# Taking the accumulators of a 5x5 convolution out through ScalarE, with the image added by TensorE

## The chip, the cores and the metric

The kernel runs on one core of a Trainium2 chip. Its time is device microseconds for one launch, from the first to the last instruction of the program. The kernel before takes 4448.21 us, the median of three runs (4447.31 to 4449.51). The profiled execution, from which all the durations below come, took 4449.83 us, of which the profile's span covers 4448.0 us.

The core has five engines that work from separate queues, each strictly in the order in which the program wrote them: TensorE (PE; the profile shows its weight loads apart, as PEld), VectorE (DVE), ScalarE (ACT), GpSimd (POOL) and SyncE (SP), which issues most of the transfers.

## The reference, cut to what matters

Four images of 128 channels and 64x64 pixels go through four residual layers. Before each layer the image is normalised in groups of four channels (`_gn`), with mean and variance over the group's channels and pixels.

```python
x = x + attention(_gn(x))          # layer 0: q, k, v of 128 channels, 4096 pixels, softmax over all of them
x = x + conv5x5(_gn(x))            # layer 1: the 5x5 convolution, 128 -> 128 channels
x = x + state_space_scan(_gn(x))   # layer 2: forward and backward scans, 64 channels x 64 states each
x = x + conv3x3(_gn(x))            # layer 3: the 3x3 convolution, with a bias
```

The change concerns the end of layer 1: the convolution's result is added to the image, and the sum and the sum of squares of the new image are taken, from which layer 2's group norm follows.

## The kernel before, in words

**Two streams of work.** The scan of layer 2 is the longest piece. It is cut into ticks, 256 for an image (`TICKS`), so 1024 for four images. A tick covers 128 rows (32 channels times 4 states) and 1024 pixels. For a tick ScalarE makes the decays (`decay`, L1246), GpSimd multiplies the drive by a row of the input matrix (`drive`, L1253), VectorE runs the recurrence (`recur`, the scan at L1263), and the result is multiplied by a row of the output matrix, on VectorE (L1266) or, for the ticks that `to_pool` gives away, on GpSimd (`weigh`, L1284). TensorE sums the products over the states (`collect`, L1304). While the decays live in one bank of 512 pixels each, there are three such banks, so `decay` can't be further ahead of `recur` than that; when image 3's operands are all made, `widen` gives two banks of 1024 pixels in their place.

**What fills the ticks.** All other work is one chain of Python generators, `images()`: for each image the attention (`attention`), the 5x5 convolution (`conv_pairs`), the operands of its scan (`scan_prep`, `scan_operands`), and, after the fourth image's operands, the end of layer 2 and layer 3 of images 0 to 2 (`stage`, `scan_end`, `conv`). The loop over `scan_core` (L1552) writes half a tick of the scan, adds half of `pace` to a credit, and draws steps from `images()` until the credit is used up. A step gives back a cost by which it is charged: `PRODUCT` = 0.86 for a product on TensorE, `SLOT` = 0.7 for a slot of operands, `HOP` = 1.7 for other steps. `pace` is 2.8 a tick until image 3's operands are made, then `ENDPACE` = 1.5. So the scan of image b is written between the attention and convolution of image b+1.

**Where the two streams meet.** The scan of image b can't be written before its first operands are. `before(b)` (L1537) is called four ticks ahead; if the operands are late, it draws the missing steps of `images()` at once, with no tick between them (it drains them). At the very end `result()` (L1545) does the same for the last transfers of image 3. `to_pool` also looks at whether operands are being made at that moment.

**The convolution.** `conv_pairs` treats two image rows at once. For each of four pieces of 1024 pixels there are three accumulators in TensorE's output memory, of 512 pixels each: `pq`, which both rows share (10 products), and `pe0` and `pe1`, for the even and the odd row (15 products each). `lean` is true for images 1 to 3. In the lean form ScalarE copies `pq` into `qs` (L975), and a product of `qs` with the identity matrix adds it to `pe0` and to `pe1` (L989). A finished accumulator isn't taken out at once: `done()` is called after the third product of the next accumulator (L966), and after the last one following a step of `HOP`. It calls `add` (L928), where VectorE adds the accumulator to the image in place and gives the sum (L930); ScalarE then gives the sum of squares into `st2` (L934, recorded at L331). The images' first, not lean, form is used for image 0 alone and is the same in both kernels.

After the last `add`, `scan_prep` aggregates the sums on VectorE (L338 to L379), GpSimd makes the scale (L381, L382), ScalarE normalises (L387), and only then TensorE can begin the taps of the short convolution (L1044).

Of the kernel before, what the change touches and what calls it, by code (L numbers as in the profile page):

```python
# [26 lines left out]
AF = mybir.ActivationFunctionType  # L27
ALU = mybir.AluOpType
# [17 lines left out]
PRODUCT, HOP, SLOT, PACE, ENDPACE, AHEAD = 0.86, 1.7, 0.7, 2.8, 1.5, 4  # L46
# [6 lines left out]
def conv_preact_kernel(  # L53
# [16 lines left out]
    nc = tc.nc  # L70
# [45 lines left out]
    ident = const.tile([P, P], F32, name="ident")  # L116
# [711 lines left out]
    def conv_pairs(b, xs, tag, st, st2, lean):  # L828

        NP, CK = H // 2, CH // W // 2  # L830
        WQ = W + PAD
        xp = large(b, f"xpe_{b}")
        rows = xp[:, : HP * WQ].rearrange("p (h w) -> p h w", w=WQ)
        xh = xs.rearrange("p (h w) -> p h w", w=W)
        nc.gpsimd.memset(rows[:, :PAD, :], 0.0)
        nc.gpsimd.memset(xp[:, (HP - PAD) * WQ : HP * WQ + PAD], 0.0)
        nc.gpsimd.memset(rows[:, PAD : HP - PAD, :PAD], 0.0)
        gn = yield from group_norm(st, f"e{b}")
        diffs = pools["big"].tile([P, VSIZE], F32, tag="V", name=f"df_{b}")
        nc.gpsimd.memset(diffs[:, 2 * (NP + 1) * WQ :], 0.0)  # L840

        def by_rows(t, n):

            return [t[:, o : o + n * WQ].rearrange("p (h w) -> p h w", w=WQ) for o in (0, PAD)]

        def piece(i):
            h0, h1 = i * H // 4, (i + 1) * H // 4
            normalise(rows[:, PAD + h0 : PAD + h1, PAD:], xh[:, h0:h1, :], gn)

        def odd(j, n):  # L850
            nc.gpsimd.tensor_tensor(
                diffs[:, j * WQ : (j + n) * WQ].rearrange("p (h w) -> p h w", w=WQ),
                rows[:, 2 * j + 1 : 2 * (j + n) : 2, :], rows[:, 2 * j + 2 : 2 * (j + n) + 1 : 2, :],
                ALU.subtract,
            )

        def even(j, n):
            at = (NP + j) * WQ
            nc.gpsimd.tensor_tensor(
                diffs[:, at : at + n * WQ].rearrange("p (h w) -> p h w", w=WQ),  # L860
                rows[:, 2 * j + 1 : 2 * (j + n) : 2, :], rows[:, 2 * j : 2 * (j + n) - 1 : 2, :],
                ALU.subtract,
            )

        wide = pools.get("fill") if not lean else None
        if wide:
            NC = NP * WQ + PAD
            combos = wide.tile([P, 3, NC], F32, tag="combos", bufs=1, name="combos")
            nc.gpsimd.memset(combos[:, :, NP * WQ :], 0.0)
            views = [by_rows(combos[:, n, :], NP) for n in range(3)]  # L870

        def combine(j, n):
            for m, (p, q, op) in enumerate(
                ((1, 2, ALU.add), (0, 2, ALU.subtract), (3, 1, ALU.subtract))
            ):
                a, b_ = (rows[:, 2 * j + r : 2 * (j + n) + r - 1 : 2, :] for r in (p, q))
                nc.vector.tensor_tensor(views[m][0][:, j : j + n, :], a, b_, op)

        def differences(i):
            last = i == 3  # L880
            if wide:
                combine(8 * i, 8)
            odd(8 * i, 8 + last)
            even(8 * i + 1, 8 + last)

        padded, differ = by_rows(xp, HP), by_rows(diffs, 2 * (NP + 1))

        def image(r, dx):
            late = dx // PAD > 0
            dx -= late * PAD  # L890
            return padded[late][:, r : r + 2 * CK - 1 : 2, dx : dx + W]

        def diff(r, dx):
            late = dx // PAD > 0
            dx -= late * PAD
            return differ[late][:, r : r + CK, dx : dx + W]

        def combo(n):
            def view(r, dx):
                late = dx // PAD > 0  # L900
                dx -= late * PAD
                return views[n][late][:, r : r + CK, dx : dx + W]
            return view

        def chunk(t, c, y):

            v = t[:, bass.ts(c, CH)].rearrange("p (h t w) -> p h t w", t=2, w=W)
            return v[:, :, y, :]

        def flat(t):  # L910
            return t.rearrange("p (h w) -> p h w", w=W)

        piece(0)
        yield HOP / 2
        piece(1)
        differences(0)
        K5 = 5
        steps, done = [], None
        taps5 = more[0] if wide else exchange(b)[:, : NTAP * C].rearrange("p (k c) -> p k c", c=C)

        def matrix(w, dx):
            if w < SUM12:
                return taps5[:, w * K5 + dx, :]
            if w < HSUM:
                return cs[:, (w - SUM12) * K5 + dx, :]
            return more[1][:, w - HSUM, dx, :]

        def add(c, y, acc):  # L928
            i = 2 * c + y
            nc.vector.scalar_tensor_tensor(  # L930
                chunk(xs, c, y), flat(acc), 1.0, chunk(xs, c, y), ALU.mult, ALU.add,
                accum_out=st2.sum(i),
            )
            st2.squares(i, chunk(xs, c, y), xs[:, 0:1])  # L934

        for c in range(L // CH):
            j = c * CK
            if c < 2:
                piece(2 + c)
            if c < 3:  # L940
                differences(c + 1)
            accs = [
                (bank("s", f"pq_{b}_{c}"), ((SUM12, image, 2 * j + 2), (SUM34, image, 2 * j + 4))),
                (bank("a", f"pe0_{b}_{c}"),
                 ((0, image, 2 * j), (1, diff, j), (3, diff, j + 1))),
                (bank("z", f"pe1_{b}_{c}"),
                 ((0, image, 2 * j + 1), (2, diff, NP + j + 1), (4, diff, NP + j + 2))),
            ]
            if wide:
                total, first, last = (combo(n) for n in range(3))  # L950
                accs = [
                    (accs[0][0], (accs[0][1][1], (HSUM, total, j))),
                    (bank("y", f"pm_{b}_{c}"), ((HDIF, diff, j),)),
                    (accs[1][0], ((0, first, j), (3, diff, j + 1))),
                    (accs[2][0], ((2, last, j), (4, diff, NP + j + 2))),
                ]
            for n, (acc, parts) in enumerate(accs):
                k, total = 0, len(parts) * K5
                for w, view, r in parts:
                    for dx in range(K5):  # L960
                        k += 1
                        nc.tensor.matmul(  # L962
                            flat(acc), matrix(w, dx), view(r, dx),
                            start=k == 1, stop=k == total and (n == 0 or not lean),
                        )
                        if k == 3 and done is not None:  # L966
                            done()
                            done = None
                        if k % 3 == 0:
                            yield 3 * PRODUCT  # L970
                if n == 0:
                    qs = pools["bg"].tile([P, MM], F32, tag="w", bufs=4, name=f"q_{b}_{c}")

                    def done(acc=acc, qs=qs, c=c):
                        nc.scalar.copy(qs, acc)  # L975
                        for y in range(0 if lean else 2):
                            nc.gpsimd.tensor_tensor(
                                chunk(xs, c, y), chunk(xs, c, y), flat(qs), ALU.add
                            )
                    yield PRODUCT  # L980
                elif wide and n == 1:
                    def done(acc=acc, c=c):
                        for y, op in enumerate((ALU.subtract, ALU.add)):
                            nc.vector.tensor_tensor(
                                chunk(xs, c, y), chunk(xs, c, y), flat(acc), op
                            )
                else:
                    if lean:
                        nc.tensor.matmul(acc, ident, qs, start=False, stop=True)  # L989
                        yield PRODUCT  # L990

                    def done(acc=acc, c=c, y=n - len(accs) + 2):
                        add(c, y, acc)
        yield HOP
        done()
        ready.add((b, "convolved"))
# [379 lines left out]
    def program(safe):  # L1376
# [118 lines left out]
        with ExitStack() as es, tc.manual_schedule():  # L1495
# [49 lines left out]
            def result():  # L1545

                while (B - 1, "staged") not in ready:
                    next(work)
                return ends[B - 1][2]

            credit = 0.0
# [91 lines left out]
```

## Time and profile before

| | us |
|---|---|
| median of three runs | 4448.21 |
| profiled execution | 4449.83 |
| span of its profile | 4448.0 |
| PE busy in the span | 3922.3 (88%) |
| DVE busy | 3722.6 (84%) |
| POOL busy | 3637.1 (82%) |
| ACT busy | 2398.0 (54%) |

The busy times are averages over stages that differ. For this change the stages of the lean images count: for image 1 the products of attention start between 732 and 1365 us, those of the convolution between 1398 and 1560 us, and the operands are made from about 1567 to 1666 us; images 2 and 3 repeat that. From about 3550 us on the last scan runs with the ends of the other images.

A matmul of fp32 operands shows as two MATMUL records, each with a duration of some 0.59 us, and the next begins 0.43 us after the last: a product takes about 0.85 us of TensorE. Counts of PE records are therefore twice the number of products.

### The profile page before, as it was taken

What the parts mean: (1) busy time and instruction counts of PE and PEld (TensorE: products, weight loads), DVE (VectorE), ACT (ScalarE), POOL (GpSimd) and SP (SyncE); (2) the same over time, 40 slices, a digit from 0 to 9 for tenths busy, and PEclk for the clock granted to TensorE, in tenths of its full rate; (3) what the DMA queues carried; (4) which work ended last, traced back from release to release, by engine and by line L of the source; (5) the groups of instructions that cost most, each with busy time, mean ns of one, the idle gap of its engine ahead of it and who ended that gap; (6) DMA issues with size and microseconds to landing.
All of it is one profiled execution on the core that took longest, in us unless ns stands there. A gap on an engine that the chain in (4) does not pass through costs nothing. (4 is left out here: it accounts for less than half of the span.)

```text
span 4448.0 us, 43613 instructions
## 1 busy us (share of the span) xinstructions
PE 3922.3 (88%) x13480; PEld 1492.0 (34%) x13480; DVE 3722.6 (84%) x3703; ACT 2398.0 (54%) x4425; POOL 3637.1 (82%) x1728
## 2 busy tenths in 40 slices
PE   8999997999999979999999889999999657576666
PEld 4444433333333323333333333333333112121222
DVE  4722217999999978999999889999999899999995
ACT  3333226666665476666664576666654754444532
POOL 3433307999999978999999889999999899999995
PEclk9999999999999989999999989999999869787887
DMA  1000016545545565455545565455445666656562
GB/s 64 21 1 1 0 55 230 182 163 178 178 173 177 178 228 195 173 178 173 182 167 173 205 228 178 166 178 179 169 178 178 225 217 208 229 199 232 189 228 78
DMA packets 213171, 726.10 MB, mean 163 GB/s; under 512 B 25152, under 2 KB 26432, under 8 KB 212672
## 3 DMA queue, kind: packets, MB, share of 16 engines
q1 hardware_dynamic: 211328, 722.49, 46.0%
q8 instruction: 108, 1.77, 0.2%
q14 instruction: 135, 1.11, 0.1%
q10 hardware_dynamic: 1600, 0.73, 0.1%
HBM read 653.98 MB, written 69.14 MB: 163 GB/s over the span
## 5 line engine op out<-in xcount | busy, mean ns | idle before, releaser
L1253 POOL TENSOR_TENSOR db<-dx,br 128x1024 f32<-128x1024 f32 x1024 | 2398.3, 2365 | 219.5 <-DMA dx<-dxd 59.5
L1246 ACT ACTIVATE da<-de,a_neg 128x512 f32<-128x512 f32 (+1 forms) x1796 | 1343.9, 751 | 741.7 <-DVE da L1263 435.5
L482 PE MATMUL sc<-r,x 128*128 128x512 f32 x2048 | 1080.8, 610 | 11.1 <-ACT last L1279 5.2
L494 PE MATMUL acc<-exchange,v 128*128 128x512 f32 x2048 | 1050.2, 595 | 2.2
L1284 POOL TENSOR_TENSOR hc<-hc,cr 128x1024 f32<-128x1024 f32 x401 | 947.9, 2364 | 17.8 <-ACT last L1279 15.3
L1266 DVE TENSOR_TENSOR hc<-da,cr 128x512 f32<-128x512 f32 (+1 forms) x1078 | 835.5, 775 | 66.8 <-DVE da L1263 0.5
L488 ACT ACTIVATE exchange<-sc 128x512 f32<-128x512 f32 x1024 | 603.2, 589 | 513.6 <-PE sc L482 508.3
L1304 PE MATMUL y<-hc,sel 128*32 128x512 f32 x4096 | 606.4, 647 | 261.6 <-POOL hc L1284 248.7
L1263 DVE TENSOR_TENSOR_SCAN da<-da,last,db 128x512 f32<-128x512 f32 (+1 forms) x464 | 728.3, 1570 | 17.2 <-POOL db L1253 14.7
L1263 DVE TENSOR_TENSOR_SCAN da<-da,da,db 128x512 f32<-128x512 f32 x455 | 585.5, 1287 | 14.9 <-ACT da L1246 14.4
L482 PEld LDWEIGHTS sc<-r,x 128*128 128x128 f32 x2048 | 363.1, 190 | 579.7 <-issue 383.8
L494 PEld LDWEIGHTS acc<-exchange,v 128*128 128x128 f32 x2048 | 387.2, 190 | 499.5 <-issue 479.3
L1263 DVE TENSOR_TENSOR_SCAN hc<-da,last,db 128x512 f32<-128x512 f32 (+1 forms) x304 | 455.7, 1499 | 2.3 <-POOL db L1253 0.7
L1263 DVE TENSOR_TENSOR_SCAN hc<-da,hc,db 128x512 f32<-128x512 f32 x317 | 406.7, 1283 | 43.5 <-ACT da L1246 13.8
L536 POOL TENSOR_TENSOR sidep<-sidep,exchange 128x512 f32<-128x512 f32 x120 | 170.9, 1424 | 273.3 <-ACT exchange L488 271.0
L1304 PEld LDWEIGHTS y<-hc,sel 128*32 128x32 f32 x4096 | 114.6, 112 | 692.4 <-POOL hc L1284 342.1
L536 DVE TENSOR_TENSOR sided<-sided,exchange 128x512 f32<-128x512 f32 x120 | 95.9, 799 | 221.5 <-ACT exchange L488 220.1
L1263 DVE TENSOR_TENSOR_SCAN da<-da,db 128x512 f32<-128x512 f32 (+1 forms) x159 | 235.8, 1483 | 11.3 <-ACT da L1246 7.3
L696 PE MATMUL pcm<-xpm,cs 128*128 128x512 f32 x432 | 211.7, 639 | 35.8 <-ACT xpm L387 35.8
L516 PE MATMUL zp<-exchange,ones 128*32 128x512 f32 x1536 | 205.6, 600 | 11.6 <-DVE xs L583 11.6
L962 PE MATMUL pe<-df,exchange 128*128 128x512 f32 x480 | 213.7, 595 | 0.0
L1279 ACT COPY last<-da 128x1 f32<-128x1 f32 x474 | 73.9, 156 | 254.3 <-DVE hc L1266 251.8
(241 smaller groups left out, 2851.1 us busy)
## 6 DMA issues: line engine op xcount, KB each, us to landing
br<-bm SPq DMA_DIRECT2D x512, 512.0 KB, 5.2
cr<-cm SPq DMA_DIRECT2D x512, 512.0 KB, 3.9
de<-dd SPq DMA_DIRECT2D x64, 512.0 KB, 4.9
dx<-dxd SPq DMA_DIRECT2D x64, 512.0 KB, 6.4
x<-in_x_dram SPq DMA_DIRECT2D x16, 512.0 KB, 5.2
xs<-in_x_dram SPq DMA_DIRECT2D x16, 512.0 KB, 6.1
xsd<-xs SPq DMA_DIRECT2D x16, 512.0 KB, 6.5
xcd<-xc SPq DMA_DIRECT2D x16, 512.0 KB, 3.0
```

What stands on the lines that cost most here:

```text
L482: nc.tensor.matmul(sc, xn[:, bass.ts(j, P)], rq[blk], start=True, stop=True)
L488: nc.scalar.activation(pt, sc, AF.Exp)
L494: nc.tensor.matmul(acc[blk], v[:, j, :], ring[:, u % NRING, :], start=j == 0, stop=j == NJT - 1)
L536: eng.tensor_tensor(s, s, ring[:, u % NRING, :], ALU.add)
L696: nc.tensor.matmul(acc.rearrange("p (r w) -> p r w", w=W), weights[:, t, :], xp[:, y : y + RPM, dx : dx + W], start=t == 0, stop=t == k * ...
L962: nc.tensor.matmul(flat(acc), matrix(w, dx), view(r, dx), start=k == 1, stop=k == total and (n == 0 or not lean),)
L1246: nc.scalar.activation(da, rep["de", b, c, d, g][:, bass.ts(h, size)], AF.Exp, scale=a_neg[:, at(i)])
L1253: nc.gpsimd.tensor_tensor(dbs[i], rep["dx", b, c, d, g], rows["b", b, c, d, q], ALU.mult)
L1263: nc.vector.tensor_tensor_scan(h, da, db[:, cut], before, ALU.mult, ALU.add)
L1266: nc.vector.tensor_tensor(hc[:, cut], h, rows["c", b, c, d, q][:, cut], ALU.mult)
L1284: nc.gpsimd.tensor_tensor(hcs[i], hcs[i], rows["c", b, c, d, q], ALU.mult)
L1304: nc.tensor.matmul(y[r : r + SG, :], sel, hcs[first + gg][:, bass.ts(h, MM)], start=q == back, stop=False, tile_position=(0, r), skip_grou ...
```

## The change

In the lean form, which is that of images 1, 2 and 3, `add` no longer uses VectorE. TensorE adds the image itself to each accumulator, by one more product with the identity matrix, and ScalarE copies the accumulator over the image and gives its sum in the same instruction. The step that holds these products is charged for two of them. `result()` accepts that the generator ends while it draws from it.

```diff
         def add(c, y, acc):
             i = 2 * c + y
-            nc.vector.scalar_tensor_tensor(
-                chunk(xs, c, y), flat(acc), 1.0, chunk(xs, c, y), ALU.mult, ALU.add,
-                accum_out=st2.sum(i),
-            )
+            if lean:
+                nc.scalar.activation(
+                    chunk(xs, c, y), flat(acc), AF.Identity, accum_out=st2.sum(i)
+                )
+            else:
+                nc.vector.scalar_tensor_tensor(
+                    chunk(xs, c, y), flat(acc), 1.0, chunk(xs, c, y), ALU.mult, ALU.add,
+                    accum_out=st2.sum(i),
+                )
             st2.squares(i, chunk(xs, c, y), xs[:, 0:1])
...
                     if lean:
-                        nc.tensor.matmul(acc, ident, qs, start=False, stop=True)
-                        yield PRODUCT
+
+                        nc.tensor.matmul(acc, ident, qs, start=False, stop=False)
+                        nc.tensor.matmul(
+                            flat(acc), ident, chunk(xs, c, n - 1), start=False, stop=True
+                        )
+                        yield 2 * PRODUCT
...
                 while (B - 1, "staged") not in ready:
-                    next(work)
+                    next(work, None)
                 return ends[B - 1][2]
```

## The prediction

> **What bounds the kernel now.** I read the page first, its sums and its slices, to see which engines have room at all.
>
> ```profile
> PE 3922.3 (88%) x13480; PEld 1492.0 (34%) x13480; DVE 3722.6 (84%) x3703; ACT 2398.0 (54%) x4425; POOL 3637.1 (82%) x1728
> PE   8999997999999979999999889999999657576666
> DVE  4722217999999978999999889999999899999995
> POOL 3433307999999978999999889999999899999995
> ```
>
> From slice 7 on three engines are near full together; only ACT has room. The dips in slices 14-15, 22-23 and 31 are where the operands of images 1 to 3 are made. Next, the busy time by engine in the three lean convolutions.
>
> ```profile
> core 0: us, PE busy (x) PEld busy (x) DVE busy (x) ACT busy (x) POOL busy (x), PEclk, DMA share, GB/s
> 1398.00:1562.00 164.00, 162.49 (x514) 63.94 (x512) 157.55 (x166) 74.71 (x118) 160.13 (x72) 1.00 0.52 176
> 2345.00:2508.00 163.00, 162.76 (x526) 63.17 (x524) 156.17 (x164) 73.06 (x115) 158.97 (x71) 1.00 0.49 172
> 3287.00:3450.00 163.00, 161.16 (x513) 63.16 (x511) 157.58 (x166) 73.69 (x117) 159.69 (x72) 1.00 0.50 180
> ```
>
> PE is busy in 99% of it, POOL in 98%, DVE in 96%. For DVE I then read its waits in the first of them: all of them together are 2.2 us, so its missing 4% is the short space between dependent instructions, and DVE is full too.
>
> ```profile
> DVE hc L1263 <- ACT da L1246: 1.0, 3, 0.3
> DVE da L1263 <- ACT da L1246: 0.8, 1, 0.8
> DVE da L1263 <- POOL db L1253: 0.4, 1, 0.4
> ```
>
> Is PE really full, when its busy time is modelled? The timeline says so: between two groups of y (L1304), which come every four ticks, 12.38 us pass from 1545.13 to 1557.51; the 24 records between them at 0.43 us and the y group at 1.92 us make 12.3. A tick there takes 3.41 us (45 GpSimd drives in 153.4 us). Last I read the timeline where image 1's convolution ends.
>
> ```profile
> 1559.36 1.12 PE L989 MATMUL pe<-q,ident 128*128 128x512 f32 x2
> ...
> 1567.10 0.67 DVE L930 SCALAR_TENSOR_TENSOR xs<-pe,xs 128x512 f32<-128x512 f32 x1
> ...
> 1567.87 0.72 ACT L331 ACTIVATE junk<-xs,aw_s 128x512 bf16<-128x512 f32 x1 [2.54 <-DVE xs L930]
> ...
> 1568.71 0.17 DVE L338 TENSOR_REDUCE gn_sums<-su_s 128x2 f32<-128x16 f32 x1 [0.94 <-ACT junk L331]
> ...
> 1573.44 1.97 PE L1044 MATMUL pt<-xn,wtap 128*64 128x512 f32 x3 [12.96 <-ACT xn L387]
> ```
>
> PE has finished the last accumulator at 1560.5, DVE comes to the add only at 1567.1, behind two ticks of scan in its queue, and PE stands idle for 13 us.
>
> **What the Trainium skill says.** Its page FP8 and Floating Point Precision, section TensorE Precision Notes, has true fp32 as four passes through the array; the trace's 0.85 us for 512 columns fits. Perfetto Trace Analysis, section Optimizing Scalar/DVE Operations, says that work which either engine can do may be moved to ScalarE if DVE is saturated. That speaks for the change, but here TensorE pays for it, and TensorE is just as full. ScalarE: Activation LUTs, section What ACT_TABLE_LOAD costs, gives 0.833 ns an element plus a fixed part for any function. The trace has the new instruction nearly exactly, in the later use of the same form (L1369, Identity with a sum): 0.668 us and 0.190 us for its accumulator.
>
> **The change part by part.** There are 8 adds in each of three images, so 24.
>
> Removed from DVE: 24 x (0.681 + 0.083) us = 18.3 us (the row of L930).
>
> Added to ACT: 24 x (0.668 + 0.190), overlapping by about 0.09, so some 0.77 each, 18.5 us. ACT is busy 75 of 164 us there, so the sum is covered. Its place isn't: the exps of the next ticks (L1246) queue behind it, and DVE needs them. At 1547 the new add would follow the exp that ends at 1547.19, with the squares (0.91) to 1548.88, where the next exp began at 1548.61. DVE, without its own 0.76, would come to that decay at 1548.4 and have it at about 1549.4: a stall of 1.0 us against 0.76 saved. So I count DVE's relief as nearly used up in the worst case, and useful only as slack.
>
> Added to PE: 24 products x 0.85 = 20.4 us, 6.8 an image. Each step is charged 0.86 more, 6.9 us of credit an image, which at 2.8 a tick is 2.5 more ticks of scan written inside the convolution. The order of the two programs shows two more in each image (55 for 53). Their y products cost 2 x 0.48 us (1.92 for four ticks). PE had 1.5 us of idle in 164, which I don't count. So the products of the convolution take **7.8 us longer** an image, +23.4 in all. DVE needs 2 x 3.29 us for the ticks (3.41 less 0.12 of adds) less 6.1: as long as before. POOL needs 160 + 2 x 3.27 (7 multiplications of 2.34 us in 5 ticks) = 166.7 in 171.8: room. PE alone decides.
>
> The handover at the end: the accumulator waited 6.6 us for DVE. When PE takes 7.8 us longer and DVE doesn't, that lag shrinks; ACT then does the add (0.77) and the squares (0.91) without a crossing. At least 1.6 us are saved (ACT idle from 1565.3 could do both by 1567.0, where DVE's aggregation, at 1568.7 now, could start), at most some 6.6. I take **4 us** an image, -12.
>
> Making the operands: here ticks are lost. The program has 15, 17 and 18 ticks between the end of the convolution and the last operand, where it had 17, 18 and 18. `before` drains 30, 12 and 7 steps (half of them operand slots, half steps of the next image's start) where it drained 10, 0 and 0. From the last add to the last GpSimd drive this stage takes 98.6, 95.3 and 94.4 us: with fewer ticks it isn't shorter, since ACT's chain (88 us of ACT durations in it) and waits between ACT, PE and DVE set it. Image 1, with one tick fewer than image 2, was even 3.3 us longer. Bounds for three lost ticks: -4.2 (the two exps of a tick, 1.4 us) to +10 (3.3 each). I take **+2**.
>
> The last scan: of the six ticks that moved into the convolutions, three come from the operands and three from the last stage, which begins at tick 773 and not 770. There a tick takes 3.2 us by DVE (2.34 for the scan, and 1.22 for the product in two of three) or POOL (4 x 2.36 / 3 = 3.15), with DVE busy 485 of 500 us between 3800 and 4300. So **-9.6**.
>
> Minor parts: five ticks go from POOL to DVE for their product (396 pooled for 401), 6 us of DVE against 12 of POOL, mostly in the operand stage, where both have gaps: 0, or up to +6. SP: the last transfer of `yt` for piece 7 now stands behind the last row load, which was issued at 4360.97; it would land by about 4367, and TensorE's last y group waits for GpSimd until 4377, so nothing is late. `result()` draws only the last transfer's steps: 0. Attention keeps its 184 ticks: 0.
>
> Sum: 23.4 - 12 + 2 - 9.6 = **+3.8 us** on the profiled 4449.83. On the median of the runs, which is 1.6 lower, 4452.0.
>
> **The rivals.** A, the sum above: 4452, chance 0.50.
>
> B, DVE sets the pace after all, and PE's products find room. Then the convolutions take no longer for two more ticks each, and the handover (-4.8 at least) and the last scan (-9.6) remain, with -1.5 in the operands: -16, 4432. For it: DVE waits for almost nothing. Against it: nor does PE, and its new work has nowhere to go. Chance 0.12.
>
> C, slower: the drained steps are laid bare. The extra ones are 20 + 12 + 7 = 39 steps, 19.5 of them operand slots. In image 1's drain now, DVE does no scan for 11.4 us, from 1615.2 to 1626.7; 5.4 us of that are the next image's statistics, so five slots cost 1.2 us each. Bare, 19.5 x 1.2 = +23; with A's other parts (+1.8) it ends at 4473 if none is won back by ticks that no longer compete. It decides the sign beyond 0.2% once more than a third of it stays bare. For it: image 1 against image 2. Against it: the same slots had to run anyway, on an ACT that was the limit with ticks between. Chance 0.22, at about 4465.
>
> D, ACT's queue becomes the wait: the exps behind each add stop DVE for 1.0 us, and PE, whose y products wait for the scan, stops too, 24 times at some 0.4 us uncovered: +10 beside A's, 4461. Against it: DVE has some 8 us of slack an image. Chance 0.16.
>
> That the change doesn't do what it says can be left out: the program has the products and activations in place.
>
> **How the numbers follow.** What a measurement can tell from no change is 0.2%, 8.9 us. A ends faster, the same or slower with 0.02, 0.40 and 0.08; B with 0.09, 0.03 and 0; C with 0, 0 and 0.22; D with 0, 0.07 and 0.09. So 0.11, 0.50 and 0.39. The time is A's, 4452. A's own range is 4442 to 4461 (handover 1.6 to 6.6 an image, operands -4 to +10, partly cancelling). The range to 4470 takes in most of C, and from 4438 down only half of B is left out.
>
> **What would show it.** In the convolutions: DVE waits for ACT's da longer than 2.2 us in all, PE without a gap, and the stretch from first to last product 6 to 8 us longer (B: unchanged). At the handover, PE's idle time before L1044 at 9 us and not 13. In the operands, 95 to 101 us from the last add to the last drive (C: above 103). From there to the end of the scan about 10 us less for image 3. The prediction is wrong if the convolutions don't grow, or if the operands grow by more than 5 us.

## The result, and the profile after

The kernel after takes 4438.07 us in the median of 14 runs (4433.87 to 4441.11), the kernel before 4447.29 us in as many on the same chip (4444.33 to 4453.03). The ratio is 0.9981, with a 95% interval from 0.9973 to 0.9988: 5 to 12 us are gained, about 8.4. The forecast was 3.8 us lost, and the most likely outcome no measurable difference. The profiled execution took 4433.9 us, its span 4431.6. The profiled execution of before lies above the middle of its runs and that of after at the low end of its own, so I profiled both programs a second time (4447.33 and 4439.43 us) and use means of two where a few microseconds count. Two profiles of one program differ by up to 5 us in the last stage and by 2.5 to 3.5 in one stretch of attention.

The page of the kernel after: busy sums of the engines, and the span in 40 slices.

```profile
PE 3931.9 (89%) x13528; PEld 1497.6 (34%) x13528; DVE 3706.3 (84%) x3670; ACT 2414.3 (54%) x4476; POOL 3622.9 (82%) x1723
PE   8999997999999989999999989999999748566667
DVE  3712217999999978999999989999999899999996
POOL 2433207999999968999999879999999799999995
```

PE has 48 records more, which are the 24 products, and 9.6 us more of busy time (in the second profiles 24.9 more, 3932.1 for 3907.2, so this sum can't price the products); DVE has 16.3 us less, ACT 16.3 more, POOL 14.2 less. The picture of the slices is the same: three engines near full, with dips where operands are made.

The busy time by engine in the three convolutions. As in the prediction's windows, a stretch begins some 13 to 17 us after the first product (image 1's first product starts at 1384.9 us in both kernels, not at 1398) and ends about 1 us past the last:

```profile
core 0: us, PE busy (x) PEld busy (x) DVE busy (x) ACT busy (x) POOL busy (x), PEclk, DMA share, GB/s
1398.00:1569.00 171.00, 171.00 (x543) 67.31 (x542) 163.68 (x162) 83.88 (x138) 170.39 (x77) 1.00 0.51 175
2341.00:2510.00 169.00, 167.50 (x539) 65.44 (x537) 160.66 (x157) 81.14 (x134) 167.11 (x76) 1.00 0.51 176
3283.00:3455.00 172.00, 170.64 (x546) 66.66 (x544) 164.39 (x162) 82.66 (x137) 170.97 (x77) 1.00 0.49 172
```

They are longer, as forecast. PE is as full as before (99 to 100%; counted from the first product to the end of the last, 175.6 of 175.9 us for image 1 before and 182.8 of 182.8 after), and DVE is no emptier (95 to 96%): what the adds left has been filled by the two more ticks. DVE's waits in the first of them show no new one behind ACT:

```profile
DVE da L1272 <- ACT da L1255: 0.9, 1, 0.9
DVE da L1272 <- POOL db L1262: 0.8, 3, 0.4
```

They add up to 1.7 us, where they were 2.2; in the other two the waits for ACT are 1.1 and 1.0 us, for 0.9 and 1.4 before. Lines of the scan stand 9 later than before (L1263 is L1272), and the new activation is L931, the new product L996. Their groups, as one line's instructions: shortest, median and longest in ns, then first and last start.

```profile
L931 ACT ACTIVATE xs<-pe x24: 573/580/599, 1415.6 to 3456.1; 128x512 f32<-128x512 f32 x24
L931 ACT ACTIVATION_READ_ACCUMULATOR xs<-pe x24: 189/193/198, 1416.1 to 3456.6; 128x1 f32 x24
L996 PE MATMUL pe<-xs,ident x48: 592/592/593, 1414.5 to 3453.0; 128*128 128x512 f32 x48
```

The activation takes 0.580 us, not the 0.668 of L1369 that I used (that row also adds a bias column). The timeline where image 1's convolution ends (start, duration, instruction, and in brackets the idle time before it and what ended it):

```profile
1566.44 1.02 PE L996 MATMUL pe<-xs,ident 128*128 128x512 f32 x2
...
1570.78 0.69 ACT L1255 ACTIVATE da<-de,a_neg 128x512 f32<-128x512 f32 x1 [2.51 <-DVE da L1272]
1571.41 0.58 ACT L931 ACTIVATE xs<-pe 128x512 f32<-128x512 f32 x1
...
1572.95 0.17 DVE L338 TENSOR_REDUCE gn_sums<-su_s 128x2 f32<-128x16 f32 x1 [1.48 <-ACT junk L331]
...
1578.56 2.73 PE L1053 MATMUL pt<-xn,wtap 128*64 128x512 f32 x4 [8.52 <-ACT xn L387]
```

The last accumulator is complete at 1567.5, yet ACT takes it out at 1571.4. The add no longer stands behind the scan in DVE's queue, but it stands in ACT's queue behind an exp which waits 2.51 us for the scan to free a bank of decays. The lag is shorter (PE waits 8.5 us for the taps instead of 13.0), not gone.

To see where the time went I cut the span by stages: the convolution from its first to its last product's start; the add lag from there to the start of the last add; the handover from there to the first tap; the operands from the first tap to the start of the last drive (L1112, one drive later than the prediction's count ended); attention from there to the next convolution. Means of two profiles each, in us:

| | image 1 before, after | image 2 before, after | image 3 before, after |
|---|---|---|---|
| convolution | 175.2, 181.9 | 177.5, 184.5 | 175.2, 184.2 |
| add lag | 7.2, 4.6 | 7.9, 4.9 | 7.5, 3.1 |
| handover | 6.3, 7.2 | 6.4, 6.3 | 6.4, 6.3 |
| operands | 95.6, 91.7 | 92.7, 91.9 | 93.2, 94.2 |
| attention of the next image | 657.8, 655.7 | 659.5, 658.4 | |

From image 3's last drive to the drive of the last tick 817.6 us became 801.8, and from there to the end 77.6 became 73.9.

A second cut goes by the scan's ticks, from GpSimd's drive (L1253, after L1262) of one tick to that of another, so that the same scan work stands in each row. Single profiles, us:

| ticks | what falls there | before | again | after | again |
|---|---|---|---|---|---|
| 192 to 300 | image 1: convolution, operands | 438.1 | 436.4 | 435.3 | 438.7 |
| 446 to 560 | image 2: the same | 451.3 | 451.8 | 449.7 | 452.6 |
| 740 to 820 | image 3: end of convolution, operands | 314.0 | 314.1 | 305.8 | 307.3 |
| 820 to 1023 | last scan | 651.6 | 655.4 | 653.5 | 654.3 |
| after 1023 | tail | 77.9 | 77.3 | 74.3 | 73.5 |

Images 1 and 2 come out level. Nearly all the gain, 11.2 of the 12.5 us by which the spans differ, stands at the end of image 3 (7.5 us) and in the tail (3.7).

### The profile page after: what moved, and what is told of

The parts are those of the page before. It is cut to its first block, busy times and chain, and to the rows that moved or that the text cites. A ratio compares the mean times of both kernels' runs of the same rounds, so it can differ in the third digit from the quotient of the medians.

```text
span 4431.6 us, 43732 instructions
## 1 busy us (share of the span) xinstructions
PE 3931.9 (89%) x13528; PEld 1497.6 (34%) x13528; DVE 3706.3 (84%) x3670; ACT 2414.3 (54%) x4476; POOL 3622.9 (82%) x1723
## 5 line engine op out<-in xcount | busy, mean ns | idle before, releaser
L1262 POOL TENSOR_TENSOR db<-dx,br 128x1024 f32<-128x1024 f32 x1024 | 2397.5, 2364 | 183.4 <-DMA dx<-dxd 53.2
L1293 POOL TENSOR_TENSOR hc<-hc,cr 128x1024 f32<-128x1024 f32 x396 | 935.5, 2362 | 20.1 <-ACT last L1288 17.0
L1272 DVE TENSOR_TENSOR_SCAN da<-da,last,db 128x512 f32<-128x512 f32 (+1 forms) x469 | 734.6, 1566 | 18.3 <-POOL db L1262 14.7
L1272 DVE TENSOR_TENSOR_SCAN da<-da,da,db 128x512 f32<-128x512 f32 x462 | 594.5, 1287 | 13.0 <-ACT da L1255 12.2
L1272 DVE TENSOR_TENSOR_SCAN hc<-da,last,db 128x512 f32<-128x512 f32 (+1 forms) x299 | 449.3, 1503 | 1.2
L1272 DVE TENSOR_TENSOR_SCAN hc<-da,hc,db 128x512 f32<-128x512 f32 x313 | 401.6, 1283 | 39.0 <-ACT da L1255 9.0
L1272 DVE TENSOR_TENSOR_SCAN da<-da,db 128x512 f32<-128x512 f32 (+1 forms) x159 | 233.7, 1470 | 11.6 <-ACT da L1255 6.8
L1288 ACT COPY last<-da 128x1 f32<-128x1 f32 x474 | 73.9, 156 | 248.1 <-DVE hc L1275 245.6
```

The lines of the kernel that those rows point to most:

```text
L1262: nc.gpsimd.tensor_tensor(dbs[i], rep["dx", b, c, d, g], rows["b", b, c, d, q], ALU.mult)
L1272: nc.vector.tensor_tensor_scan(h, da, db[:, cut], before, ALU.mult, ALU.add)
L1293: nc.gpsimd.tensor_tensor(hcs[i], hcs[i], rows["c", b, c, d, q], ALU.mult)
```

## The experiments

The diff does three things: it moves ticks (through the charge), puts products on PE, and takes adds off DVE. The first experiments do these apart; all ratios are to the kernel before on the same chip, with 95% intervals. The medians come from several chips, so they are compared by these ratios.

### The ticks alone, the engines' work alone, and the add left on VectorE

Only the charge, in the kernel before (`charge_only`; `next(work, None)` comes with it here and in the other kernel that changes the charge of before):

```diff
                         nc.tensor.matmul(acc, ident, qs, start=False, stop=True)
-                        yield PRODUCT
+                        yield 2 * PRODUCT
```

> The kernel before, with the last products of an accumulator charged for two (2 x 0.86) though there is only one; nothing else of the change. The ticks then stand exactly where the changed kernel has them (55 in each lean convolution, drains of 30, 12 and 7 steps). Theory 1, VectorE's relief is what gained: without it the convolutions pay two more ticks of 3.41 us each (+20), the last scan gives back 9.6 to 14 and the operands up to 4.5, so +2 to +6 us, 4449 to 4453. Theory 2, it is the moved ticks that gained (ticks that leave the making of operands and the last scan for a place where they cost less): most of the 9 us is here too, 4437 to 4441.

Only the work of the engines, in the kernel after (`no_charge`), with the ticks where they were:

```diff
-                        yield 2 * PRODUCT
+                        yield PRODUCT
```

> The changed kernel, charged for one product as before: both products and ScalarE's add are there, the ticks stand as in the kernel before. Theory 1, VectorE set the pace in the lean convolutions and was relieved by 18.3 us: the same gain or more, 4430 to 4440, with the convolutions' stretch at most 3 us longer than before. Theory of the forecast, TensorE sets the pace there: the stretch grows by 6.8 us an image with no ticks to show for it, less some 3 at the handover, so +11, 4458. Theory 2, the moved ticks gained: no gain, 4447 or above.

All of it but DVE's relief (`dve_takes`): VectorE takes the accumulator out, adding a tile of zeros.

```diff
-                nc.scalar.activation(
-                    chunk(xs, c, y), flat(acc), AF.Identity, accum_out=st2.sum(i)
+                nc.vector.scalar_tensor_tensor(
+                    chunk(xs, c, y), flat(acc), 1.0, flat(zeros), ALU.mult, ALU.add,
+                    accum_out=st2.sum(i),
                 )
```

> The changed kernel, with the accumulators of the lean images taken out by VectorE and not by ScalarE (the old instruction, which adds a tile of zeros in place of the image): two products, the charge for two, VectorE's 18.3 us as before. Theory 1, VectorE's relief gained: 4450 to 4456, which is the changed kernel and 12 to 18. If only TensorE counts in the convolutions, VectorE's add costs no more than the 3 us an image of the handover: up to 4447. Theory 2: 4438 to 4442.

| | ticks moved | product on PE | add | median us | ratio | convolutions 1, 2, 3 | add lags |
|---|---|---|---|---|---|---|---|
| before | no | no | DVE | 4447.29 | 1 | 175, 177, 175 | 7.2, 7.9, 7.5 |
| charge_only | yes | no | DVE | 4444.84 | 0.9997 [0.9988, 1.0005] | 179, 184, 183 | 10.5, 8.0, 7.8 |
| no_charge | no | yes | ACT | 4451.47 | 1.0013 [1.0006, 1.0019] | 182, 182, 182 | 0.6, 0.7, 3.0 |
| dve_takes | yes | yes | DVE | 4451.01 | 1.0009 [1.0000, 1.0017] | 183, 187, 185 | 7.8, 6.3, 6.0 |
| after | yes | yes | ACT | 4438.07 | 0.9981 [0.9973, 0.9988] | 182, 185, 184 | 4.6, 4.9, 3.1 |

Neither of the two theories holds alone: `charge_only` lies between what they asked for, `no_charge` refutes the first, and `dve_takes`, inside the first one's range and 9 us above the second's, refutes the second. Moved ticks alone are worth nothing that can be measured, the engines' work alone costs about 5.8 us, and together they gain 8.4. In the convolutions one sees why: the ticks alone lengthen them by 4 to 8 us, the products alone by 4 to 7, and both together by 7 to 9, hardly more than one of them. The busy times in the convolutions of `no_charge` have the other half of it:

```profile
1398.00:1567.00 169.00, 169.00 (x530) 66.77 (x528) 157.54 (x156) 80.18 (x134) 164.18 (x74) 1.00 0.49 171
2348.00:2517.00 169.00, 163.08 (x516) 64.30 (x514) 157.29 (x164) 79.28 (x134) 160.31 (x75) 0.99 0.54 176
3286.00:3455.00 169.00, 164.78 (x521) 64.62 (x519) 155.56 (x155) 80.09 (x135) 161.10 (x74) 1.00 0.49 168
```

With PE's products and without more ticks, DVE has 11.5 to 13.4 us left over in each 169, which buy nothing. In the kernel after it has 7 to 8, and two ticks more are done. (The second and third of these windows run 7.5 and 4 us past the last product, where PE waits for the next stage. From the first product to the end of the last, PE is busy for all but 0.3 us in each image of `no_charge`, and DVE has 13 to 14 us left, for 9 to 11 after.) The windows of `dve_takes` show PE and DVE full as well, but each convolution is some 1 to 2 us longer than after's, and DVE comes late to the last add again:

```profile
1398.00:1569.00 171.00, 171.00 (x544) 67.43 (x537) 163.06 (x171) 77.14 (x121) 166.17 (x75) 1.00 0.50 172
2341.00:2512.00 171.00, 169.58 (x530) 66.52 (x529) 161.37 (x169) 75.62 (x119) 165.19 (x74) 1.00 0.51 171
3283.00:3457.00 174.00, 173.29 (x551) 67.79 (x550) 165.28 (x172) 78.47 (x127) 169.42 (x77) 1.00 0.53 178
```

Between `dve_takes` and after only the engine of the add differs: 4.0 us lost became 8.4 gained. Taking 18.3 us off DVE is thus worth about 12 us, though DVE stands as full at the end as at the start. By the stages of their profiles the larger part of it is the place of the last add in a queue: the three add lags are 7.5 us shorter in after than in `dve_takes`, the three convolutions together 4.6. The advice that the prediction cites from Perfetto Trace Analysis (Optimizing Scalar/DVE Operations) holds here with a condition that only these runs show: it pays once other work of VectorE is written into the time that the product takes on TensorE.

### Which image the gain comes from

Four kernels give image 3 and images 1 and 2 apart: after's work with the charge of two in image 3 alone (`charge_last`) or in images 1 and 2 alone (`charge_first`), before's work with the charge of two in image 3 alone (`moved_last`), and the whole change in image 3 alone (`change_last`).

```diff
-                        yield 2 * PRODUCT
+                        yield (2 if b + 1 == B else 1) * PRODUCT      # charge_last
+                        yield (1 if b + 1 == B else 2) * PRODUCT      # charge_first
```

> The changed kernel, with the charge for two products in image 3 alone; images 1 and 2 are charged for one. Only the ticks of the last boundary move: out of the stretch after image 3's operands (its last operand is written at tick 774, not 770). As the forecast priced it (a moved tick pays its price in the last scan, 9.6 us for three, and nothing or a loss at the other boundaries), almost all that the charge is worth is here: 4451 less 10 to 14, so 0.997 to 0.998 of the same chip's time before plus 0.0013, that is 0.998 to 0.999. If each boundary gains alike, a third: 0.0013 less 0.001, so 1.000.

> The other two thirds: charged for two in images 1 and 2, for one in image 3. As the forecast priced it the lost ticks of the operands are worth nothing or cost 0.7 us each: 1.000 to 1.002 of before. If each boundary gains alike: two thirds of the 0.0032 between the kernel without the charge (1.0013) and the changed one (0.9981), so 0.999.

```diff
-                        yield PRODUCT
+                        yield (2 if b + 1 == B else 1) * PRODUCT      # moved_last
```

> The kernel before with one edit: in image 3 the last products of an accumulator are charged for two. No product is added, no add leaves VectorE; only ticks move, at the last boundary. In the profile of the kernel with that charge in all three images, ticks 740 to 820 take 308.8 us for 314.0 and the tail 74.2 for 77.6, and images 1 and 2 cost 2. If the changed kernel's gain is where these ticks stand, this kernel has nearly all of it: 0.9978 to 0.9988 of before, and 306 to 310 us in those ticks. If the gain needs VectorE's relief in image 3, 0.999 to 1.000.

```diff
-            if lean:
+            if lean and b + 1 == B:                                   # change_last, in add
...
+                        own = b + 1 == B
+                        nc.tensor.matmul(acc, ident, qs, start=False, stop=not own)
+                        if own:
+                            nc.tensor.matmul(
+                                flat(acc), ident, chunk(xs, c, n - 1), start=False, stop=True
+                            )
+                        yield (1 + own) * PRODUCT
```

> The whole change, products, ScalarE's adds and charge, in image 3 alone; images 1 and 2 as before. The tick windows of images 1 and 2 show no net difference between before and after, so this should be as fast as the changed kernel: 0.9975 to 0.9985. Against the kernel in which image 3 is only charged it shows what the engines' work itself gives there: 2 to 4 us if VectorE's relief counts, nothing if it doesn't. If the change gains in images 1 and 2 after all, 0.999.

| | images 1 and 2 | image 3 | median us | ratio |
|---|---|---|---|---|
| no_charge | work | work | 4451.47 | 1.0013 [1.0006, 1.0019] |
| charge_first | work, ticks | work | 4452.46 | 1.0014 [1.0007, 1.0020] |
| charge_last | work | work, ticks | 4441.09 | 0.9990 [0.9982, 0.9998] |
| moved_last | as before | ticks | 4442.44 | 0.9992 [0.9983, 1.0000] |
| change_last | as before | work, ticks | 4436.71 | 0.9982 [0.9975, 0.9990] |
| after | work, ticks | work, ticks | 4438.07 | 0.9981 [0.9973, 0.9988] |

`charge_last`, `charge_first` and `change_last` came out where the forecast's prices and the cut by ticks put them; `moved_last` didn't (0.9978 to 0.9988 and 306 to 310 us in ticks 740 to 820 were expected, 313.1 us was its window), which is the other outcome named there: the gain needs VectorE's relief in image 3. `change_last` can't be told from after, so the change in images 1 and 2 is worth nothing that these intervals, some 5 us to either side, can show, as the cut by ticks had it. In image 3 the ticks are worth about 10 us once the engines' work is done (`charge_last` against `no_charge`), which is the forecast's 9.6. But `moved_last` alone has only some 3.6 of it. The likely reason is that the ticks written earlier have to be computed earlier, on a DVE that has no room for them in before: in `moved_last` the convolution of image 3 grew to 181.8 and its add lag to 8.5; in `change_last`, with the product besides, these are 182.0 and 4.3.

### More ticks still, and the drained steps

If lost ticks in the operand stage are paid back, still more should pay too, unless the drained steps come to be bare (rival C). `charge_three` charges three products:

```diff
-                        yield 2 * PRODUCT
+                        yield 3 * PRODUCT
```

> The changed kernel, charged for three products where there are two: five ticks more than before in each lean convolution, three more than the changed kernel, drains of 50, 32 and 16 steps. If a tick in the convolution costs only its y products (0.5 us) while TensorE sets the pace, three more cost 1.5 us an image until VectorE is full again: TensorE 6.8 + 2.4 = 9.2 us longer than before, VectorE 5 x 3.29 - 6.1 = 10.4. So the convolutions grow by 2 to 4 us more an image, and what the operands give back (1 to 2 us a tick) cancels it: 0.997 to 0.999 of before. If drained steps are laid bare, as the rival C has it, the 49 more cost up to 1.2 us for each slot, +29 at most: above 1.002.

It is slower: 4467.34 us, ratio 1.0049 [1.0036, 1.0063]. The time is where C put it and not where I did. Three more ticks are written in each convolution (58 for 55), and 50, 32 and 16 steps are drained. The busy time of image 1's convolution and of its operands, in two views of `charge_three`:

```profile
1398.00:1575.00 177.00, 174.09 (x554) 67.83 (x550) 169.00 (x167) 86.22 (x141) 176.32 (x79) 1.00 0.51 178
```

```profile
1587.00:1678.60 91.60, 75.70 (x298) 28.91 (x298) 63.33 (x80) 73.76 (x122) 51.74 (x27) 0.91 0.58 202
```

and the operands of image 1 after and before, from the first tap to the last drive:

```profile
1578.60:1670.30 91.70, 75.47 (x298) 29.29 (x298) 70.99 (x87) 76.04 (x126) 60.18 (x30) 0.91 0.61 213
```

```profile
1573.40:1669.10 95.70, 77.69 (x312) 29.32 (x312) 74.53 (x90) 77.72 (x127) 70.42 (x34) 0.89 0.69 239
```

In the kernel before 15 ticks fall into that stretch, after 13, in `charge_three` 10. From 15 to 13 it gets 4 us shorter; from 13 to 10 it stays where it is, at 91.6, with 8 us less work on DVE and on POOL. For image 1 there is a floor at about 91 us, and ticks that leave below it are got back nowhere; in images 2 and 3 three ticks fewer made the stage 1.4 and 1.6 us shorter. What the extra ticks cost doesn't show where the drained steps stand, though: the operand stages are nowhere longer than in after, and by the prediction's own count they take 96.3, 95.7 and 92.8 us, where C had asked for more than 103. Of the 30 us by which the profile's span is longer than the mean of after's two, 15 stand in the three convolutions (5.5, 7.2 and 2.7) and 11 in the add lags and handovers behind them. So C's time was met, but as far as this one profile shows not by its cause: the three more ticks found no room in the convolutions. Sorted by whether image 1's two ticks were moved, whatever else was changed, the same stretch is 91.6 to 92.2 us in six profiles with and 94.1 to 95.7 in seven without.

### The tail

In the chain that ended last (start, duration, engine, tile, line), the last y group of the kernel before and the skip products behind it stand as

```profile
4377.13 3.07 PE y L1304 x8
4380.20 1.93 PE y L1315 x4
```

and those of the kernel after (six of the y group's eight records; two ran before them) as

```profile
4365.20 1.06 PE y L1313 x6
4366.26 1.03 PE y L1324 x4
```

The skip products are the same four records in both, at 1.93 and 1.03 us. The granted clock (the third column from the right) over the stretch just before and with the y group, in the kernel before and in the kernel after:

```profile
4375.00:4380.00 5.00, 2.87 (x8) 0.38 (x8) 3.13 (x2) 0.00 (x0) 2.25 (x3) 0.50 0.00 0
```

```profile
4362.00:4367.00 5.00, 4.41 (x22) 0.64 (x20) 3.06 (x2) 1.59 (x4) 2.19 (x3) 1.00 0.00 0
```

In the kernel before PE had been idle for 2.75 us when this group came, and ran at half its clock, as it had since 4370, after 4.59 us without work; in after it had just worked. Two experiments try this by giving PE products that nobody reads. `warm_tail` puts them between the last y groups of the kernel before:

```diff
+            if (b, c, d) == (B - 1, NCH - 1, 1) and q in (NQ - 3, NQ - 2):
+                idle = bank("z", f"idle_{q}")
+                for _ in range(4 if q == NQ - 3 else 2):
+                    nc.tensor.matmul(
+                        idle, ident, rows["c", b, c, d, q][:, :MM], start=True, stop=True
+                    )
```

> The kernel before, with six products that nothing reads on TensorE between its last groups of y: four after the third group from the end, two after the next. In the profile of before the last y group and the products after it ran at a granted clock of 0.50 after 2.7 to 4.6 us of idle TensorE and took 5.0 us; in the changed kernel two late products of scan_end happen to stand there and the same work took 2.1. If the clock is the reason, the tail is 74 to 75 us for 77.6 here. If it is the placement of the other work, 77 to 78.

`after_warm` puts eight into the last group norm of the kernel after, ahead of the last 3x3 convolution:

```diff
+        idle = bank("z", "idle")
+        for _ in range(8):
+            nc.tensor.matmul(idle, ident, xs[:, :MM], start=True, stop=True)
```

> The changed kernel, with eight products that nothing reads while the last group norm is made, where TensorE is idle for 8.8 us. The first 24 records of the last convolution took 12.3 and 13.3 us there, the second 24 took 10.2. If the granted clock is the reason, they take 10.2 to 10.8 here, the tail is 71 to 72 us for 74, and the time 0.9974 to 0.9976 of before, that is 2 to 3 us less than the changed kernel. If not, 0.998.

The chain of `warm_tail`:

```profile
4369.32 1.91 PE idle L1314 x4
4371.23 1.00 PE y L1304 x8
4372.23 1.03 PE y L1321 x4
```

and the granted clock from the group at 4361.3 on, the first after 4.81 us without work:

```profile
4361.00:4366.00 5.00, 4.68 (x10) 1.47 (x11) 4.89 (x4) 1.23 (x2) 2.67 (x3) 0.50 0.01 3
4366.00:4371.00 5.00, 5.00 (x18) 1.61 (x16) 3.29 (x2) 0.00 (x0) 2.42 (x3) 0.99 0.00 0
```

The same y group and skip products took 2.03 us instead of 5.00. About 1.1 of these 5.00 us was no matter of the clock: part of the group needs DVE's last product, which ended at 4378.21 in before and at 4365.15 in after. From there to the end of the skip products it is 3.9 us in before and 2.1 in after, so the clock is worth 1.8. But the tail of `warm_tail` as a whole, 77.8 us (one run, 4440.84 us), is as long as before's: the group's input was ready at 4369.38, and the products that nobody reads held it up until 4371.23. So the clock explains the durations; that it gains the tail's time isn't shown by this run. And some 2 of the tail's 3.7 us lie behind all computing. The last instruction that computes is, in before and in after,

```profile
4438.88 0.07 DVE out_of_range L1580
```

```profile
4424.73 0.06 DVE out_of_range L1589
```

From its end to that of the span pass 9.1 and 6.9 us, with the last transfer of the output and the end of the program in them. It is 8.8 to 9.2 us in the three profiles of before, before again and `warm_tail`, and 6.7 to 7.6 in all the others, those whose tail is long among them. What makes the difference is open. The tail as a whole is 72.9 to 74.4 us in all that move image 3's ticks (charge_only, dve_takes, charge_last, charge_three, moved_last, change_last) and 75.0 to 77.9 in those that don't (before, no_charge, charge_first, warm_tail).

`after_warm` took 4435.94 us, ratio 0.9979 [0.9971, 0.9988], which can't be told from after. Its first and last groups of 24 records of the last convolution, in its chain:

```profile
4383.60 12.16 PE pl L774 x24
...
4405.95 10.19 PE pl L774 x24
```

The first takes 2 us longer than the last, as in after (13.28 and, in its second profile, 12.34 us). The granted clock on both sides of its start:

```profile
4380.00:4383.60 3.60, 1.71 (x5) 0.40 (x4) 1.88 (x2) 3.20 (x3) 2.12 (x4) 1.00 0.00 0
4383.60:4386.00 2.40, 2.40 (x4) 1.15 (x5) 2.40 (x3) 0.36 (x1) 2.40 (x2) 0.62 0.00 0
```

It fell to 0.62 although PE had been busy for 6.88 us up to 1.9 us before. My expectation that the busy stretch would keep the clock up failed.

## Why the prediction was wrong

By its own terms, in us, against the means of two profiles:

| term | forecast | measured |
|---|---|---|
| convolutions | +23.4 | +22.8 |
| handover (add lag and handover) | -12 | -9.3 |
| making the operands | +2 | -3.5 |
| attention (with the stretch ahead of image 1's convolution, +0.2) | 0 | -3.0 |
| last scan | -9.6 | -15.8 |
| after the last drive | 0 | -3.7 |
| sum | +3.8 | -12.5 |

That is the whole difference of the spans in the same means; the medians of the runs differ by 9.2, the ratio gives 8.4.

**The step that failed is "Making the operands"**, with its +2, and the zero for attention that belongs to it: -6.5 us in the table, 8.5 below the forecast. The last scan (6.2 below) and the tail (3.7 below) add to the miss in the profiles, but for image 3 and the tail together the runs can't tell the forecast from the measurement, as shown below. I read from images 1 and 2 of one profile that the stage isn't shorter with fewer ticks. But these are different images with different ticks lying beside them; the right comparison is one image with and without the ticks, and no row of before could give it. Over the thirteen profiles other than `charge_three`, six with the ticks of images 1 and 2 moved and seven without, the operands of image 1 are 2.9 us shorter with two ticks fewer (91.9 for 94.9), and those of image 2 0.7 us with one tick fewer (91.9 for 92.5, with ranges that overlap); those of image 3, which lost none, are not shorter. The attention of image 2 is 3.5 us shorter (654.3 for 657.8), that of image 3 level (658.7 for 658.5). Together that is 7 us for three ticks, more than 2 a tick. Two profiles of one program differ by up to 3.5 us in that attention, so its part rests on the means of six and seven alone. My bounds for the operand stage, -4.2 to +10, held the -3.5; I took a value on the wrong side of zero and left attention out. That attention is shorter after image 1 because steps of its start had been drained is the likely reason (20 more steps are drained there, 12 for image 2), but no run shows it by itself.

The effect: images 1 and 2 were forecast at +8.9 us (7.8 - 4 + 0.7 each) and came out level in the cut by ticks and in `change_last` against after. That is 9 of the 12 us by which the runs missed the forecast. It isn't the ticks alone that did it: `charge_first` moves the ticks of images 1 and 2 in a kernel that already has the engines' work, and is no faster for it than `no_charge` (1.0014 for 1.0013). There the operands and attention are 5.6 us shorter too, but the add lags of images 1 and 2 grow by 8.6 (4.9 and 5.0 for 0.6 and 0.7). So the shorter stages are shown; how much of them reaches the total depends on the lag at the end of the convolution.

**The convolutions** were right in size and in reason: PE decides (in `no_charge` they grow by 4 to 7 us while DVE has room), and DVE's two ticks fit into what its adds left. What I didn't draw from it is that the products and the ticks lie beside each other: I charged the product's cost in full, and of six moved ticks credited the three at the end only.

**The handover** was right in kind and 2.7 us too large in sum. The crossing that I thought gone came back in ACT's queue, behind an exp that waits for the scan.

**The last scan**: on the runs the moved ticks of image 3 are worth 10 us, and 9.6 were forecast, but that they agree is in part luck. The stage is 15.8 us shorter in the profiles; the three ticks that left it, 773 to 775, stood right behind the operands in before and took 17.2 us there, 5.7 each and not 3.2. Against it stands the longer convolution of image 3, 9.0 us. By ticks, image 3 gained 7.5 us and the tail 3.7; on the runs (`change_last`, 4 to 11 us) both together gained 8, where the forecast had 5.1 for image 3 (7.8 - 4 + 0.7 - 9.6).

**The tail**, put at nothing, gave 3.7 us: 1.6 of it up to the end of the skip products, where the last y groups stand in another order and run at another clock, and 2.1 behind the last computing instruction, of which the cause is open.

**The rivals.** B's time, 4432, lies nearer than mine, but its mechanism is refuted: the convolutions did not stay as they were, they grew by 7 to 9 us. C, drained steps laid bare, isn't in this change. Its time appears one step further on, in `charge_three` (21 us over before), but not its cause: no operand stage was longer there. D isn't there: DVE waits for ACT no longer than before. Of the marks that I set, PE without a gap, its wait for the taps (8.5 us for 9), and the convolutions (6.8, 7.0 and 9.0 us for 6 to 8) were met or nearly so; the waits of DVE for ACT, which were to exceed 2.2 us, fell to 0.9 (1.8 before, without the wait for POOL); the last stage shrank by 15.8 and not about 10. The operands of image 1 by the prediction's own count, 98.6 before, were 96.6 after and inside 95 to 101: that mark was too wide to show an error made of pieces of 1 to 4 us.

What stays open: single profiles of one program differ by 2 to 5 us in the longer stages, so they are not good for smaller pieces, and `charge_first` and `charge_last` together would give 0.9991 for after by addition from `no_charge`, where 0.9981 was measured; the intervals allow that.

## What to carry to other kernels

Where two engines are full together, moving work from one to the other may pay only with a third thing that fills the room it makes: here the product on PE, with the add on ACT, cost 5.8 us alone, and gained 8.4 when scan ticks were written into the time that it took. What a tick costs where it goes has to be set against what it frees where it came from, and the latter is measured on the same stage with and without it, not on another image's. There is an end to that: the next three ticks moved in each image cost some 30 us, most of it in the convolutions and right behind them, while the operand stages gave back 3.

## What the runs showed of the hardware

The same four skip products took 1.93 us at a granted clock of 0.50 and 1.03 us at 1.00, in two programs whose work there is the same. The page TensorE: Matmul & The Clock Gate of the Trainium skill, in Part 1: The HAM clock gate, has the clock halved after about 3.4 us without work and given back after as long a stretch of work. The tail of before and `warm_tail` fit that in kind: 0.50 in before from 4370 on, after 4.59 us of idle time, with 2.75 more right before the last group; in `warm_tail` 0.50 in the first 5 us of work and 0.99 in the next 5. `after_warm` doesn't: after 6.88 us of work and 1.9 us without, the granted clock was 0.62 in the next 2.4 us. What sets it there stays open.
